# A stage border after the copy of h, and z's sum formed on its own, in a gated graph kernel

## The chip, the cores and the metric

The kernel runs on one core of a Trainium2 chip. A core has five engines that run side by side and wait for each other through semaphores: PE (matmuls), ACT (activations and copies), DVE (vector work), POOL (here: a power, and bias additions) and SP (here: transfers). The metric is the device time of one execution in microseconds, the median of three. Everything is computed in float32.

## The reference

`x` has 64 batches of 256 nodes with 128 channels, `adj` is 256 x 256. Four layers follow, each ending in a layer norm of input plus result. Layer 0 sums powers of adj applied to x, each times a weight; layer 1 is adj (x W) + b; layer 2 the same with a normalised adj. Layer 3 is a gated recurrence of five steps:

```
m_in = adj @ h;  m_out = adj @ h;  av = concat(m_in, m_out)
u3 = h @ u3_w.T + u3_b
z  = sigmoid(av @ w3_w.T + w3_b + u3)
r  = sigmoid(av @ w4_w.T + w4_b + u3)
hv = tanh(av @ w5_w.T + w5_b + ((r * h) @ u5_w.T + u5_b))
h  = (1 - z) * h + z * hv
```

Both propagations use the same adj, so `m_in` equals `m_out`, and the two halves of w3, w4 and w5 can be added once.

## The kernel before, in words

Two batches make a group: 512 nodes by 128 channels, so that one result fills one PSUM bank of 128 x 512. There are 32 groups. A group is written as a Python generator (`group`, L226 to L313) whose `yield`s are stage borders. The main loop (L316 to L329) keeps four groups running. A turn of the loop, a tick, moves each running group on by one stage, in the order in which they entered. Groups enter two ticks apart at first; when one ends, the next enters in the following tick, so the offsets persist from one round of four groups to the next. A group takes 26 ticks.

The order in which instructions are written is the priority with which a planner, at build time, fills each engine's queue. It keeps to that order except where, by its own estimate of times, an instruction's input isn't there yet; then it draws a later one ahead. PSUM has one pool of 8 banks (`bank`, L68) for all groups. [...]

A step of layer 3 holds h twice: `hT` with channels on the partitions, and `h` with nodes on the partitions, which `propagate` (L202) needs. Its stages are:

1. transposes of the last step's `hT` into a bank (L306, L215: `pth` in the profile), ACT's copy to `h` (L309), and the propagation by adj (L207: `pmg`) with ACT's copy to `m` (L209, `mg` in the profile);
2. `pr` = u3·hT + w4·m on PE, r = sigmoid(pr) on ACT (L286), rh = r * hT on DVE (L288);
3. w34·m added onto `pr`, where w34 = w3 - w4, so that the bank now holds z's sum; z on ACT (L292); `ph` = w5·m + u5·rh, hv = tanh(ph) on ACT (L297); d = hv - hT, d = z * d, hn = hT + d on DVE (L300 to L303).

All products go through `mm` (L71), so they share line L72 and are told apart by tiles. In layers 0 to 2 DVE does the norms (`residual`, L180; `normalise`, L195): the sum s, statistics st and mv, ve, then POOL raises ve to -0.5 (rs, L192), and DVE makes y from s, mv and rs (L198). POOL also adds the bias to y (yb, L220).

## Time and profile before

| | before |
|---|---|
| median of three runs | 1668.61 us (1668.55 to 1669.2) |
| profiled execution | 1668.61 us |
| its span, first to last instruction | 1666.8 us |
| PE busy | 1578.1 us, 95% |
| DVE busy | 900.8 us, 54% |
| ACT busy | 561.2 us, 34% |
| POOL busy | 216.0 us, 13% |
| mean granted PE clock | 0.984 |

Busy times are sums over instructions. PE's matmuls are pipelined and their ends are modelled, so its busy time isn't the time that it needs: the distance from one start to the next tells more. A product of 128 x 128 weights with 128 x 512 data in float32 shows as two matmul instructions.

### The profile page before, as it was taken

Reading aid. Unit: us, or ns where it says so; the run is one execution under the profiler, and the core shown is the slowest. Engines: PE = TensorE matmul, PEld = TensorE weight load, DVE = VectorE, ACT = ScalarE, POOL = GpSimd, SP = SyncE. Lnnn points to the kernel's source line nnn. Section 1 sums busy time; section 2 is a strip of 40 time slices with the busy share of each in tenths; the row PEclk is TensorE's granted clock in tenths of the full one; section 3 lists DMA queues with packets and bytes.
Section 4 is the critical chain, followed back from the end, with each engine's and each line's share of the span. In section 5 each row is a group of like instructions: output and inputs, shape, how many; then the busy total and the mean of one; then the engine's idle time right before and its main releaser. Section 6 shows DMA issues by size and latency. Waiting matters only on the chain.

```text
span 1666.8 us, 16967 instructions
## 1 busy us (share of the span) xinstructions
PE 1578.1 (95%) x6366; PEld 1011.8 (61%) x6366; DVE 900.8 (54%) x2560; ACT 561.2 (34%) x898; POOL 216.0 (13%) x199
## 2 busy tenths in 40 slices
PE   6989999899999999899998999989999899998996
PEld 4755567555675557655576555765557655585553
DVE  3654457534674356744566445664357644566346
ACT  1134421344213442144421444124431244312443
POOL 0310014000130002300023000220003200032001
PEclk9999999999999999999999999999999999999998
DMA  3000000000000001000010000100000000000000
GB/s 87 20 1 0 7 26 20 1 1 7 26 19 1 1 7 32 14 1 0 13 33 7 1 0 13 32 7 1 0 13 20 1 1 0 13 14 1 1 0 26
DMA packets 36452, 19.38 MB, mean 12 GB/s; under 512 B 2065, under 2 KB 36241, under 8 KB 36369
## 3 DMA queue, kind: packets, MB, share of 16 engines
q1 hardware_dynamic: 34064, 17.04, 3.5%
q10 hardware_dynamic: 2304, 1.25, 0.3%
q8 instruction: 50, 0.82, 0.2%
q14 instruction: 34, 0.27, 0.1%
HBM read 9.90 MB, written 8.39 MB: 11 GB/s over the span
## 4 chain that ended last, share of the span: by engine, by line
PE 77%; DVE 14%; POOL 4%; ACT 2%; issue 1%; DMA 1%; ACTq 0%; POOLq 0%; DVEq 0%
PE pr L72 24%; PE pmg L72 17%; PE ph L72 15%; PE p L72 7%; PE py L72 6%; DVE y L198 4%; PE pth L215 4%; POOL rs L192 4%; DVE st L186 3%; PE pm L72 2%; DVE s L182 2%; DVE mv L188 1%; ACT hv L297 1%; ACT h L309 1%; DVE d L301 1%
## 5 line engine op out<-in xcount | busy, mean ns | idle before, releaser
L192 POOL TENSOR_TENSOR rs<-ve,half 128x4 f32<-128x4 f32 x128 | 131.9, 1031 | 1350.5 <-DVE ve L190 1350.5
L72 PE MATMUL pmg<-aT,h 128*128 128x256 f32 x1024 | 267.3, 406 | 24.9 <-ACT h L309 24.9
L288 DVE TENSOR_TENSOR rh<-r,hT 128x512 f32<-128x512 f32 x160 | 110.0, 687 | 333.6 <-ACT r L286 333.6
L72 PEld LDWEIGHTS pmg<-aT,h 128*128 128x128 f32 x1024 | 192.7, 198 | 128.6 <-ACT h L309 103.9
L198 DVE TENSOR_SCALAR y<-s,mv,rs 128x128 f32<-128x128 f32 x512 | 165.7, 373 | 117.9 <-POOL rs L192 117.9
L300 DVE TENSOR_TENSOR d<-hv,hT 128x512 f32<-128x512 f32 x160 | 110.4, 690 | 161.8 <-ACT hv L297 161.8
L286 ACT ACTIVATE r<-pr,rb 128x512 f32<-128x512 f32 x160 | 109.9, 687 | 216.2 <-PE pr L72 216.2
L209 ACT COPY mg<-pmg 128x512 f32<-128x512 f32 x160 | 93.7, 585 | 257.4 <-PE pmg L72 257.4
L72 PE MATMUL p<-aT,x 128*128 128x256 f32 (+1 forms) x512 | 170.4, 486 | 0.0
L72 PE MATMUL pr<-hT,u3T 128*128 128x512 f32 x320 | 168.6, 609 | 0.0
L72 PE MATMUL pr<-mg,w34T 128*128 128x512 f32 x320 | 164.6, 596 | 2.7 <-ACT r L286 2.7
L297 ACT ACTIVATE hv<-ph,hb 128x512 f32<-128x512 f32 x160 | 110.0, 687 | 169.2 <-PE ph L72 169.2
L72 PE MATMUL ph<-rh,u5T 128*128 128x512 f32 x320 | 164.3, 595 | 2.1 <-DVE rh L288 1.9
L72 PE MATMUL pr<-mg,w4T 128*128 128x512 f32 x320 | 164.0, 594 | 0.0
L72 PE MATMUL ph<-mg,w5T 128*128 128x512 f32 x320 | 163.4, 592 | 0.0
L215 PEld LDWEIGHTS pth<-ident,hT 128*128 128x128 f32 x640 | 79.7, 142 | 102.8 <-issue 91.9
L292 ACT ACTIVATE z<-pr,zb 128x512 f32<-128x512 f32 x160 | 109.9, 687 | 94.9 <-PE pr L72 83.1
L72 PEld LDWEIGHTS p<-aT,x 128*128 128x128 f32 x512 | 94.8, 190 | 66.2 <-issue 61.2
L215 PE MATMUL pth<-ident,hT 128*128 128x128 f32 x640 | 98.2, 277 | 28.5 <-DVE hT L303 28.5
L301 DVE TENSOR_TENSOR d<-z,d 128x512 f32<-128x512 f32 x160 | 118.0, 738 | 4.9
L72 PEld LDWEIGHTS py<-w0s,xT 128*128 128x128 f32 x1024 | 119.5, 192 | 1.8
L72 PE MATMUL py<-w0s,xT 128*128 128x128 f32 x1024 | 119.8, 275 | 0.0
(85 smaller groups left out, 1531.3 us busy)
## 6 DMA issues: line engine op xcount, KB each, us to landing
x<-in_x_dram SPq DMA_DIRECT2D x32, 256.0 KB, 2.8
out_dram<-y SPq DMA_DIRECT2D x32, 256.0 KB, 2.3
w_raw<-in_L_gnn_weight_dram ACTq DMA_DIRECT2D x1, 448.0 KB, 4.3
a_nat<-in_adj_dram SPq DMA_DIRECT2D x1, 256.0 KB, 4.5
raw_w3T<-in_L_gnn_w_w_dram ACTq DMA_DIRECT2D x1, 128.0 KB, 5.2
raw_w4T<-in_L_gnn_w_w_dram ACTq DMA_DIRECT2D x1, 128.0 KB, 5.2
raw_w5T<-in_L_gnn_w_w_dram ACTq DMA_DIRECT2D x1, 128.0 KB, 3.1
w1s<-in_L_gnn_weight_dram ACTq DMA_DIRECT2D x1, 64.0 KB, 5.0
```

Of the source, the lines that this page charges most:

```text
L72: nc.tensor.matmul(o, lhsT, rhs, start=start, stop=stop, **kw)
L186: nc.vector.bn_stats(st[:, q, :], s[:, q, :])
L192: nc.gpsimd.tensor_tensor(rs, ve, half, op=OP.pow)
L198: nc.vector.tensor_scalar(y[:, q, :], s[:, q, :], mv[:, q, 0:1], rs[:, q:q + 1], op0=OP.subtract, op1=OP.mult)
L209: nc.scalar.copy(m, ps)
L215: nc.tensor.transpose(ps[:, q * P:(q + 1) * P], block, ident)
L286: nc.scalar.activation(r, pr, AF.Sigmoid, bias=rb, scale=1.0)
L288: nc.vector.tensor_mul(rh, r, hT)
L292: nc.scalar.activation(z, pr, AF.Sigmoid, bias=zb, scale=1.0)
L297: nc.scalar.activation(hv, ph, AF.Tanh, bias=hb, scale=1.0)
L300: nc.vector.tensor_sub(d, hv, hT)
L301: nc.vector.tensor_mul(d, z, d)
```

## The change

z's sum gets a bank of its own, `pz`, made of u3·hT and w3·m in stage 2. `w34T` and the product with it go, and `pr` isn't written again after r has been read. The stage border that stood between rh and w34's product moves behind z's activation. A new border comes after the copy to `h`, in the four steps that make that copy: transposes and copy are now a stage of their own, and the propagation comes one tick later. A group takes 30 ticks instead of 26.

```diff
-    w34T = const.tile([P, P], F32, name="w34T")
-    nc.vector.tensor_sub(w34T, w3T, w4T)
...
             rh = work.tile([P, NB * N], F32, tag="rh", name=f"rh{s}_{g}")
             nc.vector.tensor_mul(rh, r, hT)
-            yield
-            mm(pr, w34T, m, False, True, skip_group_check=True)
+            pz = bank(f"pz{s}_{g}")
+            mm(pz, u3T, hT, True, False)
+            mm(pz, w3T, m, False, True)
             z = work.tile([P, NB * N], F32, tag="z", name=f"z{s}_{g}")
-            nc.scalar.activation(z, pr, AF.Sigmoid, bias=zb, scale=1.0)
+            nc.scalar.activation(z, pz, AF.Sigmoid, bias=zb, scale=1.0)
+            yield
             ph = bank(f"ph{s}_{g}")
...
                 nc.scalar.copy(h.rearrange("p q c -> p (q c)"), pT)
+                yield
```

`mm` also loses its extra keyword arguments, which only the removed product used.

## The prediction, made before the result was known

> **What bounds the kernel now.** I read the page first: busy shares, then the chain that ended last.

> ```profile
> span 1666.8 us, 16967 instructions
> PE 1578.1 (95%) x6366; PEld 1011.8 (61%) x6366; DVE 900.8 (54%) x2560; ACT 561.2 (34%) x898; POOL 216.0 (13%) x199
> PE 77%; DVE 14%; POOL 4%; ACT 2%; issue 1%; DMA 1%; ACTq 0%; POOLq 0%; DVEq 0%
> L72 PE MATMUL pr<-mg,w34T 128*128 128x512 f32 x320 | 164.6, 596 | 2.7 <-ACT r L286 2.7
> ```

> PE is the bound; no other engine exceeds 54%. A product of 128x512 is two matmul instructions, so 320 of them are 160 products (32 groups, 5 steps). The means overlap, being pipelined, so a price must come from starts. The timeline near the end, PE alone (start, length, work), shows the repeating step:

> ```profile
> 1563.29 0.60 PE L215 MATMUL pth<-ident,hT 128*128 128x128 f32 x4
> 1563.72 1.02 PE L72 MATMUL pr<-mg,w34T 128*128 128x512 f32 x2
> 1564.70 1.99 PE L72 MATMUL pmg<-aT,h 128*128 128x256 f32 x8
> 1566.53 1.02 PE L72 MATMUL pr<-hT,u3T 128*128 128x512 f32 x2
> 1567.39 1.02 PE L72 MATMUL pr<-mg,w4T 128*128 128x512 f32 x2
> 1568.25 1.02 PE L72 MATMUL ph<-mg,w5T 128*128 128x512 f32 x2
> ```

> From start to start a 128x512 product costs 0.86 us (1566.53 to 1567.39) and four transposes 0.43. Propagation starts 0.98 after a product that costs 0.86, so 0.12 is lost, and lasts 1.83 where the unhindered one of y takes 1.73 (276.03 to 277.76). That is the h copy arriving late, although another group's product is already drawn in between. The waits (total, times, longest) and the timeline at 615 show the same wait with nothing between:

> ```profile
> PEld pmg L72 <- ACT h L309: 103.9, 128, 1.1
> PE pmg L72 <- ACT h L309: 24.9, 32, 0.8
> PE pth L215 <- DVE hT L303: 28.5, 10, 3.1
> ```

> ```profile
> 615.08 0.60 PE L215 MATMUL pth<-ident,hT 128*128 128x128 f32 x4
> 616.50 1.99 PE L72 MATMUL pmg<-aT,h 128*128 128x256 f32 x8 [0.82 <-ACT h L309]
> ```

> Here 1.42 passes instead of 0.43: 0.99 lost, and about 0.1 more inside the propagation. The third wait is another matter: once a round of four groups, DVE is late with hn of the first group's first step. PE, then DVE, then the windows with PEclk after the busy times of PE, PEld, DVE, ACT and POOL:

> ```profile
> 292.06 1.05 PE L72 MATMUL py<-w2T,m 128*128 128x128 f32 x8
> 296.25 0.97 PE L215 MATMUL pth<-ident,hT 128*128 128x128 f32 x4 [3.14 <-DVE hT L303]
> ```

> ```profile
> 292.00 1.11 DVE L198 TENSOR_SCALAR y<-s,mv,rs 128x128 f32<-128x128 f32 x4 [1.13 <-POOL rs L192]
> 293.03 0.68 DVE L300 TENSOR_TENSOR d<-hv,hT 128x512 f32<-128x512 f32 x1
> 293.75 1.64 DVE L301 TENSOR_TENSOR d<-z,d 128x512 f32<-128x512 f32 x1
> 295.42 0.69 DVE L303 TENSOR_TENSOR hT<-hT,d 128x512 f32<-128x512 f32 x1
> ```

> ```profile
> 290.00:296.30 6.30, 3.16 (x22) 2.79 (x21) 5.06 (x15) 1.27 (x2) 2.59 (x2) 1.00 0.00 0
> 296.40:303.20 6.80, 6.12 (x15) 3.98 (x15) 3.34 (x15) 1.17 (x2) 1.02 (x1) 0.50 0.00 0
> ```

> The hole lasts 3.3 us by starts; after it the clock is halved for 6.8 us. This happens in all eight rounds, for 3.4 or 6.8 us, 44 us in all, which costs 22 us of PE work.

> [...] the d at 293.03 stood behind a y that waited for rs until 292.00, while hv had ended at 290.8. [...] d took 1.64 at 293.75 beside POOL's yb, against a mean of 0.74. [...] No stall of PE here is put down to a bank.

> **The change part by part.** All against the profiled execution: span 1666.8, and 1.8 around it; its 1668.61 is also the median.

> 1. *Two products make z's sum instead of one.* w34T·m goes; u3T·hT and w3T·m come. That is one product more per step: 160 x 0.86 = **+137.6**. It is the surest term: same shape, weights, and moving operands as rows already there, on the engine that is 95% busy. Removing the subtraction that made w34T saves one small DVE instruction beside the preamble: 0. Activations are as many as before.

> 2. *z no longer continues r's sum.* In the old order the w34T product had to wait until r had been read from the bank. That stalls once a round (transposes at 320.68, product at 321.62: 0.94 instead of 0.43, and 0.1 after it): 8 x 0.6 = **-5**.

> 3. *The new border.* Program order per step becomes: propagation | r, z | ph, hv, hn | transposes, copy. Groups enter two ticks apart and a step now has four ticks, so in full flow two groups stand two stages from the other two. Between one group's transposes and its propagation another's four products come (3.44 us), where the copy needs 0.9 (0.2 to start, 0.58, 0.1). So the wait goes everywhere: 96 x (0.12 + 0.11) + 32 x (0.99 + 0.11) = 57; I take **-55**, as some fall in half clock. The other covers: rh needs 1.7 us after r's sum and has z's own 1.72 plus others; hn needs 3.3 after ph and finds 5.2 or more in full flow. No DMA or queue of SP is moved; an ACT copy stays behind its own transposes. Without this cover the 55 would stay.

> 4. *The crowded place of each round (280 to 296), where DVE and POOL set the pace.* The groups' ticks up to there are unchanged. z's sum now comes before the propagation of layer 2 that stalled at 282.95 and 285.00 (1.7 us), so its 1.72 falls into that hole; but ph's second product still waits for rh (288.93) on DVE. One 0.86 a round is hidden: 8 x 0.86 = **-7**. If DVE came sooner it would cost its full 0.86.

> 5. *The 3.3 us hole.* Taking w34T from ahead of ph makes hv ready earlier in the planner's account, so I expect it to put d before part of the four y instructions that now precede it. Then the order y, d, y, d, y, hn, y from 292.0 ends at 292.0 + 3 x 0.3 + 3 x 0.7 + gaps = 295.2, not 296.1[...]. Bounds: 0 (order unchanged) to -2.1 a round (d first of all); I take 0.9: **-7**.

> 6. *Clock.* With no copy wait inside the stretch after the hole, 3.4 us should be the rule instead of 6.8, and some rounds escape. Bounds 0 and -22; eight at 3.4 would cost 13.7 instead of 22, so -8; I take **-10**.

> 7. *Tail*: w34T's and rh's waits around 1652 go, the last hn wait stays: **-1**.

> Sum: 1666.8 + 137.6 - 5 - 55 - 7 - 7 - 10 - 1 = 1719.4; with 1.8, **1721**.

> **Rivals.** (a) *Hole and clock stay as they are*: terms 5 and 6 vanish or nearly, 1730 to 1740. For it: rs still arrives at 292.0[...]. Against it: hv's product is 0.86 earlier. (b) *The hole shrinks below what halves the clock*: term 5 -17, term 6 -22, 1699. Holes of 1.7 us at 283 to 285 are followed by full clock, so this needs d ahead of y. (c) *New waits take the place of the copy's*: two groups at the same stage send r, z and h copies in bunches to ACT, and stalls of half the old size (+28) or all of it (+55) come back: 1749 to 1776. Against it: ACT is at 34%, and covers are several us. (d) *Not slower*: by starts PE needs 1856 instructions of 512 columns at 0.43, 2048 of 256 at 0.215 and 2432 of 128 at 0.1075, together 1500 us; the other 167 are holes, slow clock, head and tail. If the added products filled these, time would hold: it decides at 137.6 recovered. But some 19 lie before layer 0's first products at 24.3, 8 after the last product at 1658, and 10 in gaps of a few ns at each of 6366 instructions; 130 remain. (e) *The border changes nothing, since the planner already draws work between*: then 128 waits stay, 1721 + 55 = 1776; the 32 bare waits speak against it.

> **How the numbers follow.** Likeliest case 0.38 (1712 to 1728); (a) 0.22; (b) 0.18; (c) and (e) 0.18, mostly the half-size form; (d) 0.02, the rest in between. The range 1694 to 1752 leaves out the far ends of (b), (c) and (e), some 0.17. Less than 0.2% from before (3.3 us) is what a measurement can't tell from no change: faster 0.01, same 0.01, slower 0.98.

> **What would show it.** Right: pz rows of 320 instructions for u3T and for w3T at 0.86 per product; no wait of pmg for the h copy worth naming, and 1.73 per propagation; no hT wait above 2.5 us; PEclk 0.50 for 3.4 us or less a round. Wrong: pz at another price, 32 or more waits of pmg near 0.8, new waits of ph for rh or pth for hT in full flow, or DVE's y still all ahead of d.

## The result, and the profile after

The changed kernel takes 1711.7 us (1711.44 to 1711.95, four runs), the kernel before 1668.9 beside it: a ratio of 1.0255, 95% interval 1.0237 to 1.0273. It is slower. The forecast was 1721, with a range from 1694 to 1752. The profiled execution has a span of 1710.2, which is 43.4 more than before. In the code after the change line numbers are one to three lower, so the transposes are L212 and hn is L302.

From the page of the kernel after: span, busy times, and two groups of PE (tiles, shapes, count, then busy time and mean of one, then PE's idle time before them).

```profile
span 1710.2 us, 17681 instructions
PE 1662.1 (97%) x6686; PEld 1069.3 (63%) x6686; DVE 893.9 (52%) x2559; ACT 562.0 (33%) x898; POOL 214.0 (13%) x199
L72 PE MATMUL pmg<-aT,h 128*128 128x256 f32 x1024 | 241.9, 379 | 0.0
...
L72 PE MATMUL pz<-mg,w3T 128*128 128x512 f32 x320 | 163.4, 592 | 0.0
```

PE has 320 more matmul instructions, which is 160 products. The propagation of h now waits for nothing, where it had 24.9 us of waits, and the mean of one of its instructions fell from 406 to 379 ns. The timeline of PE in full flow (start, length, work):

```profile
1573.67 1.02 PE L72 MATMUL pz<-hT,u3T 128*128 128x512 f32 x2
1574.53 1.02 PE L72 MATMUL pz<-mg,w3T 128*128 128x512 f32 x2
...
1577.11 1.89 PE L72 MATMUL pmg<-aT,h 128*128 128x256 f32 x8
1578.83 1.02 PE L72 MATMUL ph<-mg,w5T 128*128 128x512 f32 x2
```

The new product costs 0.86 from start to start, and the propagation 1.72, no more than the unhindered one. There is no gap. The crowded place of a round now looks like this, first on PE, then on DVE:

```profile
293.13 1.02 PE L72 MATMUL ph<-mg,w5T 128*128 128x512 f32 x2
295.20 1.12 PE L72 MATMUL ph<-rh,u5T 128*128 128x512 f32 x2 [1.04 <-DVE rh L285]
...
298.32 1.05 PE L72 MATMUL py<-w2T,m 128*128 128x128 f32 x8
300.99 0.66 PE L212 MATMUL pth<-ident,hT 128*128 128x128 f32 x4 [1.60 <-DVE hT L302]
```

```profile
298.27 0.35 DVE L195 TENSOR_SCALAR y<-s,mv,rs 128x128 f32<-128x128 f32 x1 [1.14 <-POOL rs L189]
298.53 0.69 DVE L299 TENSOR_TENSOR d<-hv,hT 128x512 f32<-128x512 f32 x1
299.13 0.34 DVE L195 TENSOR_SCALAR y<-s,mv,rs 128x128 f32<-128x128 f32 x1
299.39 0.69 DVE L300 TENSOR_TENSOR d<-z,d 128x512 f32<-128x512 f32 x1
299.99 0.34 DVE L195 TENSOR_SCALAR y<-s,mv,rs 128x128 f32<-128x128 f32 x1
300.25 0.68 DVE L302 TENSOR_TENSOR hT<-hT,d 128x512 f32<-128x512 f32 x1
```

DVE now takes y and d in turn. hn is done 2.7 us after rs arrived, where it took 4.1 (292.00 to 296.1). Some 0.95 of the 1.4 us gained belong to the second d: beside POOL's yb it took 1.64 us, now it takes 0.69, and yb starts only at 302.53, after hn. In the trace of before, the second d overlaps yb eight times and took 1.63 us or more in each, and at most 0.69 in the other 152. The eight y·w2 instructions of layer 2 cost 0.86, so the hole before the transposes is 300.99 - 298.32 - 0.86 = 1.8 us, against 3.3. In exchange ph's second product waits longer for rh: 2.07 from start to start instead of 1.21, so 0.86 more. The windows of the kernel after, with PEclk behind the five busy times:

```profile
0.00:1700.00 1700.00, 1661.46 (x6682) 1068.92 (x6682) 889.15 (x2543) 562.01 (x898) 212.97 (x198) 1.00 0.04 11
```

PE was at full clock until the tail (1702.9). Before the change, 44.4 us ran at half clock ahead of the tail.

### The profile page after: what moved, and what is told of

Its sections match the earlier page's. It is cut to its first block, busy times and chain, and to the rows that moved or that the text cites. A ratio compares the mean times of both kernels' runs of the same rounds, so it can differ in the third digit from the quotient of the medians.

```text
span 1710.2 us, 17681 instructions
## 1 busy us (share of the span) xinstructions
PE 1662.1 (97%) x6686; PEld 1069.3 (63%) x6686; DVE 893.9 (52%) x2559; ACT 562.0 (33%) x898; POOL 214.0 (13%) x199
## 4 chain that ended last, share of the span: by engine, by line
PE 81%; DVE 12%; POOL 4%; issue 1%; DMA 1%; POOLq 0%; ACT 0%; DVEq 0%
PE pr L72 15%; PE ph L72 15%; PE pz L72 15%; PE pmg L72 14%; PE p L72 7%; PE py L72 6%; PE pth L212 5%; DVE y L195 4%; POOL rs L189 3%; DVE st L183 3%; PE pm L72 2%; DVE s L179 2%; DVE mv L185 1%; POOL yb L217 1%; PE ptx L212 1%
## 5 line engine op out<-in xcount | busy, mean ns | idle before, releaser
L72 PEld LDWEIGHTS pmg<-aT,h 128*128 128x128 f32 x1024 | 194.6, 190 | 77.7 <-issue 57.4
L72 PE MATMUL pmg<-aT,h 128*128 128x256 f32 x1024 | 241.9, 379 | 0.0
L72 PE MATMUL ph<-rh,u5T 128*128 128x512 f32 x320 | 164.3, 595 | 7.9 <-DVE rh L285 7.9
L72 PE MATMUL p<-aT,x 128*128 128x256 f32 (+1 forms) x512 | 170.4, 486 | 0.0
L72 PE MATMUL pr<-hT,u3T 128*128 128x512 f32 x320 | 165.3, 598 | 0.0
L290 ACT ACTIVATE z<-pz,zb 128x512 f32<-128x512 f32 x160 | 110.0, 687 | 164.5 <-PE pz L72 164.5
L72 PE MATMUL ph<-mg,w5T 128*128 128x512 f32 x320 | 163.5, 592 | 0.0
L72 PE MATMUL pr<-mg,w4T 128*128 128x512 f32 x320 | 163.4, 592 | 0.0
L72 PE MATMUL pz<-mg,w3T 128*128 128x512 f32 x320 | 163.4, 592 | 0.0
L72 PE MATMUL pz<-hT,u3T 128*128 128x512 f32 x320 | 163.4, 592 | 0.0
L72 PEld LDWEIGHTS p<-aT,x 128*128 128x128 f32 x512 | 94.8, 190 | 66.2 <-issue 61.2
L212 PEld LDWEIGHTS pth<-ident,hT 128*128 128x128 f32 x640 | 78.7, 141 | 78.1 <-issue 51.0
L72 PEld LDWEIGHTS py<-w0s,xT 128*128 128x128 f32 x1024 | 119.4, 192 | 1.8
L72 PE MATMUL py<-w0s,xT 128*128 128x128 f32 x1024 | 119.8, 275 | 0.0
L72 PEld LDWEIGHTS ph<-rh,u5T 128*128 128x128 f32 x320 | 60.1, 190 | 87.5 <-issue 71.9
```

Of the source, the lines that this page charges most:

```text
L72: nc.tensor.matmul(o, lhsT, rhs, start=start, stop=stop)
L212: nc.tensor.transpose(ps[:, q * P:(q + 1) * P], block, ident)
L290: nc.scalar.activation(z, pz, AF.Sigmoid, bias=zb, scale=1.0)
```

## The experiments

Six kernels were run beside the kernel before, whose median was 1669.76 in the first four comparisons and 1670.38 in the last two. They ask three things. What does each half of the change do alone? Does the clock follow the hole? What shortened the hole?

### The border alone

```diff
--- before
                 nc.scalar.copy(h.rearrange("p q c -> p (q c)"), pT)
+                yield
```

> The border after the copy of h, in the kernel before; z's sum is still made from r's. My theory (PE is full, a product costs 0.86, the border takes away all copy waits, the hole of 3.3 us once a round and the halved clock stay because the four y still stand ahead of d): after minus 137, plus 12 for the longer hole, plus 7 for the hidden product, plus 14 to 18 for the clock: 1605 to 1613 us, mean clock near 0.985. Rival 'the border does nothing, the planner already draws work between': 1669. Rival 'the added products were partly hidden': closer to after than 90 us, so above 1622.

Measured: 1617.2 us (1612.63 to 1621.5), a ratio of 0.9684 with an interval of 0.9662 to 0.9706; mean clock 0.985. The rival by which the border does nothing would have given 1669, so it falls. So does the one by which the added products were partly hidden as a rule: this kernel is 94.5 below after, although it still has the long hole and the slow clock. From its waits (total, times, longest):

```profile
PE pth L215 <- DVE hT L303: 29.5, 10, 3.1
...
PE pr L72 <- ACT r L286: 6.2, 8, 0.8
```

The hole is as long as in the kernel before, and seven stretches of half clock follow, 41 us in all. The time is 4 above my upper figure. The second line shows a wait that I had left out: at one place a round w34's product now stands right behind w4's of the same group and waits for r, 0.94 us by starts, 8 x 0.94 = 7.5. So the 94.5 are the 137.6 of the added products, less 12 for the longer hole, 7 for the product that hides in the crowded place, 17 for the half clock (counted as in step 6 below) and this 7.5, which makes 94.

### The separate sums alone

```diff
--- after
                 nc.scalar.copy(h.rearrange("p q c -> p (q c)"), pT)
-                yield
```

> z's own sum without the border: the kernel after with its new border taken out. My theory: w34's product was what filled the copy wait before; without it, the transposes and the propagation of one group stand next to each other 128 times, each with a bare wait of 1.1 us: after plus 141, so 1845 to 1855 us, with 128 waits of pmg for the h copy near 0.8 us. Rival 'the copy waits are as in the kernel before' (32 bare, 96 short): after plus 55, 1760 to 1770.

Measured: 1854.1 us, a ratio of 1.1102 with an interval of 1.1086 to 1.1119. From the waits, and from the timeline of PE:

```profile
PE pmg L72 <- ACT h L308: 103.3, 128, 0.8
```

```profile
1154.58 0.60 PE L212 MATMUL pth<-ident,hT 128*128 128x128 f32 x4
1156.00 1.99 PE L72 MATMUL pmg<-aT,h 128*128 128x256 f32 x8 [0.82 <-ACT h L308]
```

All 128 propagations stand bare behind their own transposes, 1.42 us after them instead of 0.43. In the kernel before, 96 of these places were filled by w34's product of another group, the very product that the change removes. So the border is worth 1854.1 - 1711.7 = 142 us beside separate sums (with four stretches of half clock that it takes away, of 3.4 us each), but 53 us beside the old ones (1669.8 - 1617.2). The two edits can't be priced apart and added.

### A longer hole in the kernel after

Two kernels put DVE instructions that leave d as it is ahead of hn, once a round. `hole_plus1` has one of them, `hole_plus2` two.

```diff
--- after
+            if s == 0 and g % ACTIVE == 0:
+                for _ in range(2):
+                    nc.vector.tensor_tensor(d, d, d, op=OP.max)
             hn = work.tile([P, NB * N], F32, tag="hT", name=f"hT{s}_{g}", bufs=2 * ACTIVE)
```

> The kernel after with two more DVE instructions (maximum of d with itself, 0.69 us each, which leaves d as it is) ahead of hn, in the first step of the first group of each round only: eight places. The hole before the transposes grows from 1.8 to 3.2 to 4.2 us. Theory 'the hole halves the clock': half clock for 3.4 to 6.8 us after each of the eight holes, mean clock near 0.985, time 1736 to 1757. Rival 'the clock has nothing to do with the hole': clock 0.998 as in after, time plus 12 to 20 only, 1724 to 1731.

Measured: 1748.6 us, 36.9 above after; mean clock 0.985. PE's timeline, and one of the windows:

```profile
304.79 1.05 PE L72 MATMUL py<-w2T,m 128*128 128x128 f32 x8
309.98 0.48 PE L212 MATMUL pth<-ident,hT 128*128 128x128 f32 x1 [4.14 <-DVE hT L305]
```

```profile
309.00:315.80 6.80, 5.82 (x10) 2.93 (x11) 4.40 (x16) 1.27 (x2) 1.40 (x2) 0.50 0.01 2
```

The hole grew from 1.8 to 309.98 - 304.79 - 0.86 = 4.3, so by 2.5 x 8 = 20 us. Half clock came back after each of the eight holes, five times for 6.8 us and three times for 3.4. The other 17 us are what the half clock costs by the count of step 6 below. The rival with an unmoved clock, 1724 to 1731, falls.

> The kernel after with one more DVE instruction (maximum of d with itself) ahead of hn in the same eight places. hole_plus2 had holes of 4.3 us and half clock after each; after has 1.8 us and none. Here the hole should be near 2.8 us by one instruction and one y that slips ahead, up to 3.3 if the bias addition on POOL meets it. Theory 'the share of an idle stretch decides': half clock in most or all of the eight rounds, 3.4 us at a time, time 1720 to 1740, mean clock 0.987 to 0.995. [...]

Measured: 1731.6 us, 19.9 above after; mean clock 0.990. The hole is 2.7 us (302.54 - 299.02 - 0.86 = 2.66), and seven of the eight are followed by 3.4 us of half clock. The profiled execution has a span 17.9 longer than that of after: 0.86 x 8 = 7 are the hole, and 11 remain for the clock.

### w34's product behind ph, with and without the border

Is it the order of y and d on DVE that shortens the hole? Here z's sum is still made from r's, but written behind ph and hv, so that hv is ready earlier in the planner's account.

```diff
--- before, and border_alone
-            mm(pr, w34T, m, False, True, skip_group_check=True)
-            z = work.tile([P, NB * N], F32, tag="z", name=f"z{s}_{g}")
-            nc.scalar.activation(z, pr, AF.Sigmoid, bias=zb, scale=1.0)
...
             nc.scalar.activation(hv, ph, AF.Tanh, bias=hb, scale=1.0)
+            mm(pr, w34T, m, False, True, skip_group_check=True)
+            z = work.tile([P, NB * N], F32, tag="z", name=f"z{s}_{g}")
+            nc.scalar.activation(z, pr, AF.Sigmoid, bias=zb, scale=1.0)
```

> The kernel before, without the border, with w34's product and z's activation written after ph and hv. The planner then puts d behind the first y, as in after. Theory 'the order of d and y shortens the hole, and the clock follows': hole near 1.3 us, ph waits 1.2 us for rh instead of 0.35, copy waits as in before, half clock in at most half of the rounds: 1640 to 1655 us, mean clock 0.99 or more. Rival 'hole and clock came from the border': as before, 1669, clock 0.984.

Measured, without the border: 1646.95 us, a ratio of 0.9858 with an interval of 0.9843 to 0.9873, so 1.4% less; mean clock 0.994. Its waits:

```profile
PE pmg L72 <- ACT h L309: 24.9, 32, 0.8
...
PE pth L215 <- DVE hT L303: 12.2, 10, 3.0
```

The hole on PE, and what DVE does meanwhile:

```profile
290.45 1.05 PE L72 MATMUL py<-w2T,m 128*128 128x128 f32 x8
292.60 0.63 PE L215 MATMUL pth<-ident,hT 128*128 128x128 f32 x4 [1.09 <-DVE hT L303]
```

```profile
289.54 0.35 DVE L198 TENSOR_SCALAR y<-s,mv,rs 128x128 f32<-128x128 f32 x1 [1.13 <-POOL rs L192]
289.80 0.69 DVE L300 TENSOR_TENSOR d<-hv,hT 128x512 f32<-128x512 f32 x1
...
290.91 0.68 DVE L301 TENSOR_TENSOR d<-z,d 128x512 f32<-128x512 f32 x1
```

PE's copy waits are those of the kernel before, to the digit. The hole fell to 292.60 - 290.45 - 0.86 = 1.3 us, and only three rounds had a stretch of half clock, of 3.4 us. hv was ready before rs in both kernels (290.8 against 292.0 before, 288.3 against 289.5 here), so it is d's place in DVE's queue that counts, not an earlier hv. Of the 2.0 us by which the hole shrank, 1.2 come from this order (hn is done 2.95 us after rs, against 4.1). The other 0.86 is a wait that moved: ph's second product now waits for rh ahead of the place, so PE gets there 1.8 us after rs instead of 0.95. Hole and clock came from where w34's product stands, not from the border.

> border_alone with w34's product and z's activation written after ph and hv instead of ahead of them, so that the planner puts d behind the first y only. Theory: hole of 1.4 to 2.2 us instead of 3.3, so no or rare halving of the clock: 1576 to 1592 us, mean clock above 0.993. Rival 'the order of d and y is not what shortens the hole': same as border_alone, clock 0.985.

Measured, with the border: 1591.5 us, a ratio of 0.9531 with an interval of 0.9517 to 0.9546; mean clock 0.997. PE's timeline:

```profile
284.99 1.05 PE L72 MATMUL py<-w2T,m 128*128 128x128 f32 x8
287.14 0.63 PE L215 MATMUL pth<-ident,hT 128*128 128x128 f32 x4 [1.10 <-DVE hT L303]
```

The hole is 287.14 - 284.99 - 0.86 = 1.3 us, and the clock stays full until 1580 us. This version beats both kernels: it has the border and the shortened hole, and keeps one product for z instead of two.

## Why the prediction was right

The direction and the place of each wait were right, and the 9 us between 1721 and 1711.7 come from the sizes of terms, not from a mechanism that failed. Even so 1711.7 lies a little below the band of the case called likeliest (1712 to 1728): the clock did what rival (b) had said.

The right column is counted by starts over both traces. At full clock an instruction of 512 columns is given 0.43 us, one of 256 columns 0.215 and one of 128 columns 0.1075, at half clock twice as much (median distances in the trace of before: 0.429, 0.216 and 0.109 us, at half clock 0.853, 0.426 and 0.213); what is left until the next start is idle time.

| step | predicted | counted |
|---|---|---|
| 1 two products instead of one | +137.6 | 160 x 0.86: +137.6 |
| 2 wait of w34's product for r | -5 | no such wait left: -5 |
| 3 border: copy waits | -55 | no wait of pmg for h left: -53 |
| 4 one product a round hidden | -7 | pm wait gone, 13; ph's wait for rh longer, 7: -6 |
| 5 the hole | -7 | 3.3 to 1.8 us, 8 x 1.5: -12 |
| 6 the clock | -10 | all half clock before the tail gone: -18.5 |
| 7 tail | -1 | one wait for hT of 1.6 us more, others gone: about 0 |
| sum on the span | +52.6 | +43.1; the spans differ by +43.4 |

- **Step 1** stands on the rows of the kernel after, and on border_w34_last: with one product for z it is 120 us below after, although waits in the crowded place that the second product had covered are back there (13.9 us in the propagations of layer 2, by starts, against 0.6 in after). The products were paid in full, 0.86 us each, wherever PE wasn't waiting anyway.
- **Step 3** is shown by the waits, and by the two halves alone. The forecast said "Without this cover the 55 would stay" of a missing border. That was too low for this change. Without w34's product as filler 128 bare waits would stand there, worth 142 with the half clock that they bring. The sum wasn't touched by it, since the border was there. Rival (e), by which the border does nothing and the time is 1776, rested on the same figure.
- **Step 4**: the propagation that stalled for 1.7 us runs through, and the wait went to rh, as forecast.
- **Step 5** is the first term that was mis-sized. The order y, d, y, d, y, hn came as described. I had put the end of hn 0.9 us sooner than before. It came 1.4 us sooner after rs (2.7 us against 4.1), since the instructions on DVE here start before the one ahead has ended in the records (y at 298.27 lasts 0.35, the d behind it starts at 298.53, so 0.09 sooner): three y, two d and hn took 2.7 us, where I had added gaps to full lengths. PE reaches the place 0.9 us after rs in both, so the hole is 1.5 shorter.
- **Step 6** is the second, and the larger. I took "3.4 us should be the rule", an estimate of mine: before had it in three rounds of eight, 6.8 in the others. In the kernel after, a hole of 1.8 us was not followed by half clock once in eight rounds. The forecast's bound of 22 took PE to be busy all through the 44 us at half clock. By the count it was idle for 7.4 of these 44.4 us, so about (44.4 - 7.4) / 2 = 18.5 us were lost, and all of them came back. The same count gives 11 us for hole_plus1 and 17 for hole_plus2; with their longer holes, 7 and 20, that is about 18 and 37, and their spans are 17.9 and 37.8 longer than that of after. Two of the eight rounds held 2.05 us of idle time within 3.4 us, against 2.23 or more where half clock followed, as the last section shows.

Rival (b), clock at full speed for good, was right about the clock but tied it to a shorter hole and so to 1699. Rival (a), hole and clock unchanged, came true in border_alone, where w34's product stayed ahead of ph. Rival (c), new waits in full flow, did not appear: in the kernel after, pth waits for hT ten times and ph for rh eight times, that is, once a round and in the tail. Rival (d) needed 137.6 us recovered; 94 were.

## What to carry to other kernels

On PE, 95% busy here, an added product cost its distance from start to start, 0.86 us, and a saved wait paid its own length, and more only where the clock stayed up with it: 12 us of shorter holes brought 18 us of clock with them. 137.6 stood against 94. Before taking work out, look where the planner had used it as filler: the product removed here was what hid the copy that the new border then had to hide. A stage border, together with one product moved behind another so that the planner puts the work that is waited for first, gave 4.7% here without any added work.

## What the hardware showed that was not expected

The length of a hole alone did not tell whether half clock followed. A hole of 1.8 us was followed by it in no round of eight (after), one of 2.7 in seven (hole_plus1), one of 3.3 in eight in the kernel before but only in seven in border_alone, one of 4.3 in eight (hole_plus2). After a hole of 1.8 with a bare copy wait of 0.9 right after the transposes it came in four rounds (sums_alone), after 1.3 with the same wait in three (w34_last_alone).

```profile
285.57:288.98 3.41, 1.58 (x12) 1.31 (x10) 2.91 (x6) 0.59 (x1) 2.01 (x2) 1.00 0.00 0
288.98:292.39 3.41, 2.10 (x8) 1.29 (x9) 3.34 (x12) 0.59 (x1) 0.00 (x0) 1.00 0.00 0
...
483.54:486.95 3.41, 1.34 (x6) 0.90 (x7) 3.34 (x6) 0.59 (x1) 0.65 (x1) 1.00 0.00 0
486.96:490.37 3.41, 3.41 (x7) 1.87 (x6) 2.24 (x13) 0.69 (x1) 1.02 (x1) 0.50 0.02 5
```

In the second round the hole is split between two steps, with PE busy for 1.58 and 2.10 us of 3.41, and the clock stays. In the third, one step has PE busy for 1.34 us only, and the next is slow. Two rounds of the kernel after held 2.05 us of idle time by starts in one step (at 508.21 and 1344.48), and the clock stayed. How the chip itself counts idle time isn't shown, and these figures belong to this count and these traces.
